# Reordering the table steps and the weighing of rows in a two-layer graph kernel on one core

## Chip, core and metric

The kernel runs on one core of a Trainium2 chip. Time is the device time of one execution in microseconds (us), and less is better. The core's engines run side by side, each through its own instruction stream in order: PE (TensorE, matrix products and transposes), DVE (VectorE), ACT (ScalarE), POOL (GpSimd) and SP (SyncE, which here only issues transfers). Transfers between the chip's DRAM (HBM) and the on-chip memories (SBUF, and PSUM for PE's results) run on 16 DMA engines.

## What is computed

There are 32 items; each is a matrix x of 512 channels by 1024 nodes. Two layers follow each other, each with a residual sum and a layer normalization over the nodes.

```python
# layer 0: attention over nodes, then a linear map and ReLU
q = einsum('c,bcn->bn', wq, x);  k = einsum('c,bcn->bn', wk, x)
scores = q[:, None, :] + k[:, :, None]
scores = where(scores > 0, scores, 0.01 * scores)
att = softmax(scores, axis=-1)
agg = einsum('bcn,bmn->bcm', x, att)
x = layernorm(x + relu(einsum('oc,bcm->bom', adj, agg) + bm[None, :, None]))
# layer 1: a linear map with W = adj * adj
x = layernorm(x + einsum('bnf,nm->bmf', x, adj * adj) + bias)
```

## The kernel before

**The attention without its 1024 x 1024 matrix.** A score is q of one node plus k of another, through a leaky ReLU, so after sorting the nodes by q the exponentials of a row split at one place: on one side they are exp(q) times a factor of the row, on the other exp(0.01 q) times another. Sums from the front and from the back of the sorted nodes therefore give every row of the attention. For an item b the steps are:

- `project` (L259): PE multiplies x by the weights and gets z = adj x with q and k as extra columns, in eight parts of 128 nodes, each in two halves; ACT copies each part into `zrow` (L275). Their PSUM tiles come from `ps_mm`, which has three buffers.
- `place` (L319), `send` (L333), `fetch` (L372): DVE counts each node's rank, POOL scatters the rows of z into a DRAM table `td` at their ranks, and SP fetches them back sorted into `zs` with eight transfers, the first six of which hold what the first weights need.
- `weigh` (L389): ACT takes exponentials of the sorted q (L398) and DVE multiplies them with triangular masks into `lq` (L406, L414), which are PE's weights for the tables. Part 0 gives the weights for table steps 0 and 1, part 1 those for all others.
- `table` (L418), nine steps: PE makes running sums of 120 sorted rows (`tp`, L426), ACT copies them out (L431), POOL and ACT carry the last sum into the next step's input (L435, L437), and SP writes the sums to `td` (L440). A step cannot start before the carry of the step before. Most steps share one PSUM buffer, `ps_t`.
- `pick` (L444): POOL gathers for 128 nodes at a time the row at its split and the two sums beside it, into `rows`; eight gathers an item.
- `shares` (`own` and `norm`), `scale`, `gain` (L456 to L504): small DVE operations and an exponential on ACT give three factors for each node; ACT scales the first row by its factor (L493), DVE adds the two others (L501, two instructions a gain).
- `turn` (L535): eight PE transposes bring 128 channels back, ACT applies bias and ReLU (L543). `join` adds x (L548) and takes statistics (`stats`, L510, L512); `root`, `shift` and `apply` normalize, on POOL (L518, L519), DVE (L525) and ACT (L531).

**Layer 1** is one level of a Strassen-Winograd scheme: `sums` (L575) builds differences of the normalized halves in parts of `rows` that are free by then, seven pairs of products (`mul`) run on PE (L592), and DVE adds them up (`read`, L604). `stats1`, `roots`, `ready` normalize the result and store it. For the last item some sums and additions run on POOL.

**The order.** Nothing is rearranged by a scheduler: the order of the calls is the order on each engine, and waits follow from the data and from buffers. `begin` and `opening` fill the pipeline, then `slot(s)` runs for s = 1 to 29. In slot s, item s+2 is projected while the tables of item s+1 (`mid`) are made, item s's last rows (4 to 7) are weighed and turned, and item s-1 (`old`) is normalized. Then `phase` runs the layer-1 products of item s, ranks and scatters item s+2, gathers rows for item s+1 and weighs its rows 0 to 3. So that the engines overlap, the calls of a slot are spread by hand over the eight projections z = 0 to 7 (L869 to L934). The first table step of item s+1 stands between the two halves of projection 4.

`end` (L936) has the last two items, 30 (`s`) and 31 (`mid`), with no projection left: the rows 4 to 7 of item 30 and the tables of item 31, the layer-1 products of item 30 (`rest`, L654, with `after(i)` called behind each product), the gathers and weighing of item 31, and `last` for its layer 1.

Of the kernel before, what the change touches and what calls it, by code (L numbers as in the profile page):

```python
# [23 lines left out]
def gat_gcn_resnorm_kernel(  # L24
# [46 lines left out]
    nc = tc.nc  # L71
# [505 lines left out]
    def layer1(b):  # L577
# [19 lines left out]
        def read(mt, half, w, m, *of):  # L597
            if (b, mt) not in vs:
                pool, tag = (xpool, "x") if b >= B - 2 else (vpool, "v")
                vs[b, mt] = pool.tile([P, N], F32, name=f"v_{b}_{mt}", tag=tag)  # L600
            x0 = ops[b, w][:, m, :] if w else vs[b, mt][:, half]
            x1 = bias_bc[:, half] if not of else vs[b, of[0]][:, of[1]]
            by = nc.gpsimd if b == B - 1 and not w else nc.vector
            by.tensor_tensor(vs[b, mt][:, half], x0, x1, ALU.add)  # L604

        mul, get = [], {}
# [47 lines left out]
    def rest(b, after):  # L654

        mul, get, reads = layer1(b)
        names = (("c1",), ("c5",), ("u2",), ("u3", "u4", "22"), ("21",), ("12",), ("11",))
        for i in range(len(mul)):
            mul[i]()
            if i == 0:  # L660
                after(-1)
                shift(0, b, CT - 1)
                apply(0, b, CT - 1)
                sums(b, ("T2", 0), ("T2", 1), ("T3", 0), ("T3", 1), ("T4", 0), ("T4", 1))
            for name in names[i // 2]:
                if b == B - 1 and i > 9:
                    get[name, i % 2]()
                elif i % 2:
                    reads(name)
            after(i)  # L670
# [198 lines left out]
    def slot(s):  # L869
# [4 lines left out]
        for z in range(NT):  # L874
            step, ot = 2 * (z - tz), z - tz
            if z == NT - 1:
                turn(s, CT - 1)
                sums(s, ("T1", 0), ("T1", 1))
            project(new, z, 0)
            if step >= 0:  # L880
                table(mid, step)
            if ot == 0:
                roots(old, 0, 1)
            if ot == 1:
                root(0, s, 0)
            if ot == 2:
                roots(old, 2, 3)
            if z == NT - 1:
                add(s, CT - 1)
            if 0 <= ot < CT - 1:  # L890
                turn(s, ot)
            if z == NT - 1:
                shift(0, s, CT - 2)
                apply(0, s, CT - 2)
            project(new, z, 1)
            if z == 0:
                shares(s, NT // 2, NT)
                scale(s, (4, 5))
                gain(s, (4, 5))
            if z == 1:  # L900
                scale(s, (6, 7))
                gain(s, (6,))
            if z == 2:
                weigh(mid, 0)
                gain(s, (7,))
            if z == 3:
                stats1(old, 0, 1)
            if step == 0:
                weigh(mid, 1)
            if step >= 0:  # L910
                table(mid, step + 1, pool=ps_mm if z == NT - 1 else ps_t)
            if step == 4:
                share(mid)
            if 0 <= ot < CT - 1:
                join(s, ot)
                if ot > 0:
                    root(0, s, ot)
            if ot == 0:
                for mt in (0, 1):
                    shift(1, old, mt)  # L920
                    apply(1, old, mt, by=nc.vector)
                    store(old, mt)
            if ot == 1:
                stats1(old, 2, 3)
            if ot == 2:
                for mt in (2, 3):
                    shift(1, old, mt)
            if new + 1 < B and z >= tz:
                load(new + 1, ot)
# [6 lines left out]
    def end():  # L936

        s, mid, old = B - 2, B - 1, B - 3
        shares(s, NT // 2, NT)
        scale(s, range(NT // 2, NT))  # L940
        gain(s, (4, 5))
        weigh(mid, 0)
        table(mid, 0)
        gain(s, (6,))
        table(mid, 1)
        gain(s, (7,))
        weigh(mid, 1)
        for ot in range(CT):
            turn(s, ot)
            if ot == CT - 1:  # L950
                sums(s, ("T1", 0), ("T1", 1))
            table(mid, 2 + ot)
            join(s, ot)
            root(0, s, ot)
        share(mid)

        def after(i):
            if i in (-1, 2, 4):
                table(mid, CT + 2 + (i + 1) // 2)
            if i in (5, 7):  # L960
                ready(old, i - 5, i - 4)
            if i in (3, 5):
                stats1(old, i - 3, i - 2)
                roots(old, i - 3, i - 2)
            if i == 5:
                for mt in range(6):
                    pick(mid, mt)
            if i in (7, 9):
                pick(mid, 6 + (i - 7) // 2)

        rest(s, after)
        shares(mid, 0, 2)
        scale(mid, (0, 1))
        own(mid, 2, 4)
        gain(mid, (0,))
        norm(mid, 2, 4)
        scale(mid, (2, 3))
        gain(mid, range(1, 4))
        shares(mid, 4, NT)
        scale(mid, range(4, NT))  # L980
        gain(mid, range(4, NT))
        for ot in range(CT):
            turn(mid, ot)
            if ot == CT - 1:
# [39 lines left out]
```

## Time and profile before

| What | Value |
|---|---|
| Median of 3 runs | 2340.5 us (2339.24 to 2347.45) |
| The profiled execution | 2344.84 us, its span 2342.9 us |
| Mean granted PE clock | 0.977 |
| Bytes moved by DMA | 548.68 MB, 234 GB/s over the span |

The span is the time from the first to the last instruction in the profile of one execution. The page also shows how the engines' work lies over the span, in 40 slices of 58.6 us; a digit is the busy share of a slice in tenths:

```profile
PE   8869999999999999999999999999999999999666
DVE  4278988988898988898898899898889889889777
ACT  2565566666556667556667655666655666755443
POOL 1334444543444543444453344454344445334333
PEclk9979999999999999999999999999999999999787
DMA  6567878777778777777777787877778787777741
```

PE is busy nearly throughout from the fourth slice on; the last three slices, about 176 us, are less filled on all engines and on the DMA. The chain of work that ended last, as shares of the span:

```profile
DVE 55%; DMA 13%; issue 10%; PE 9%; ACT 7%; POOL 5%; SPq 0%; ACTq 0%; DVEq 0%; POOLq 0%
```

The slots follow each other about every 69 us. A line of the timeline has the start, the duration, the engine, the line of the kernel, the operation, out<-in by the names of the tiles, the shapes and the count, and in brackets the idle time ahead of it with what ended it. A line of the waits has the total in us, the number of times and the longest.

### The profile page before, as it was taken

To read this page: it belongs to the slowest core of one execution; us is meant where nothing else is said; L and a number is where in the kernel's file an instruction comes from. 1 tells how busy PE (TensorE), PEld (TensorE's weight loads), DVE (VectorE), ACT (ScalarE), POOL (GpSimd) and SP (SyncE) were. 2 spreads that over 40 slices of the span, in tenths; PEclk is the share of its full clock that TensorE was granted. 3 is DMA by queue.
4 is the path that set the end of the run, shared out by engine and by line. 5 is a ranking of instruction groups with operands and counts; after the bars stand their busy time and mean duration, and the time that the engine had idled before them with its cause. 6 is when DMAs were issued, how large, how long until landed. Compare 5 with 4: busy or idle time off the path is not lost.

```text
span 2342.9 us, 30955 instructions
## 1 busy us (share of the span) xinstructions
PE 2200.9 (94%) x9521; PEld 1385.4 (59%) x9521; DVE 1995.4 (85%) x4156; ACT 1402.6 (60%) x2186; POOL 1001.9 (43%) x1299
## 2 busy tenths in 40 slices
PE   8869999999999999999999999999999999999666
PEld 7636666566666656666556665565666665666322
DVE  4278988988898988898898899898889889889777
ACT  2565566666556667556667655666655666755443
POOL 1334444543444543444453344454344445334333
PEclk9979999999999999999999999999999999999787
DMA  6567878777778777777777787877778787777741
GB/s 250 164 196 236 258 239 275 253 223 226 247 246 263 259 234 221 237 255 245 265 239 221 238 250 241 271 253 227 228 237 257 253 264 243 224 232 232 218 173 72
DMA packets 175421, 548.68 MB, mean 234 GB/s; under 512 B 24748, under 2 KB 24760, under 8 KB 175256
## 3 DMA queue, kind: packets, MB, share of 16 engines
q1 hardware_dynamic: 117888, 277.18, 39.7%
q0 software_dynamic: 57344, 269.52, 32.8%
q8 instruction: 76, 1.25, 0.2%
q14 instruction: 89, 0.73, 0.1%
q10 hardware_dynamic: 24, 0.01, 0.0%
HBM read 338.17 MB, written 208.43 MB: 233 GB/s over the span
## 4 chain that ended last, share of the span: by engine, by line
DVE 55%; DMA 13%; issue 10%; PE 9%; ACT 7%; POOL 5%; SPq 0%; ACTq 0%; DVEq 0%; POOLq 0%
DVE lt L326 13%; DMA rows<-td,idx 10%; DVE v L604 9%; DVE st L510 8%; DVE rows L501 6%; PE zp L267 5%; DVE rows L575 5%; DVE y L548 4%; PE tp L426 3%; POOL td L336 3%; DVE v L533 2%; PE op L539 2%; ACT y L531 2%; ACT y L543 1%; DVE lq L406 1%
## 5 line engine op out<-in xcount | busy, mean ns | idle before, releaser
L267 PE MATMUL zp<-wmT,x 128*128 128x257 f32 x4096 | 947.0, 383 | 2.6 <-ACT zrow L275 2.6
L267 PEld LDWEIGHTS zp<-wmT,x 128*128 128x128 f32 x4096 | 757.1, 190 | 164.0 <-issue 37.2
L435 POOL COPY zs<-ts 1x513 f32<-1x513 f32 x256 | 175.0, 683 | 803.4 <-ACT ts L431 803.1
L426 PE MATMUL tp<-zs,lq 128*64 128x257 f32 x2304 | 328.4, 400 | 83.8 <-DVE lq L406 66.2
L501 DVE SCALAR_TENSOR_TENSOR rows<-rows,ra 128x512 f32<-128x512 f32 x512 | 373.0, 750 | 35.2 <-ACT rows L493 26.1
L447 POOL DMA_INDIRECT rows<-td,idx x256 | 292.1, 1141 | 202.3 <-issue 119.4
L336 POOL DMA_INDIRECT td<-zrow,ranki x256 | 277.6, 1084 | 117.7 <-DVE ranki L331 47.9
L469 ACT ACTIVATE ac<-s 128x4 f32<-128x4 f32 (+1 forms) x65 | 13.6, 209 | 501.5 <-DVE s L468 413.6
L326 DVE SCALAR_TENSOR_TENSOR lt<-qb,zrow,first 128x1024 int8<-128x1024 f32 x240 | 307.2, 1280 | 4.3
L426 PEld LDWEIGHTS tp<-zs,lq 128*64 128x64 f32 x2304 | 150.1, 139 | 243.3 <-DVE lq L406 72.6
L431 ACT COPY ts<-tp 128x514 f32<-128x514 f32 x288 | 169.1, 587 | 193.4 <-PE tp L426 184.0
L351 ACT ACTIVATE sg<-lq,kc 128x1024 int8<-128x1024 f32 x240 | 275.8, 1149 | 6.8
L592 PE MATMUL oA<-y,adj_sb 128*128 128x512 f32 x512 | 245.1, 612 | 7.0 <-ACT y L531 4.7
L592 PE MATMUL oS<-rows,ws 128*128 128x512 f32 x512 | 225.5, 592 | 0.0
L493 ACT ACTIVATE rows<-rows,ra 128x512 f32<-128x512 f32 x256 | 167.7, 716 | 56.7 <-DVE ra L480 48.6
L275 ACT COPY zrow<-zp 128x514 f32<-128x514 f32 x256 | 148.1, 579 | 82.4 <-PE zp L267 70.9
L519 POOL TENSOR_TENSOR rs<-rs,mhalf 128x1 f32<-128x1 f32 x256 | 171.8, 671 | 21.3
L531 ACT ACTIVATE y<-y,nb,rs 128x1024 f32<-128x1024 f32 x128 | 158.7, 1240 | 27.8 <-DVE nb L525 26.3
L539 PE MATMUL op<-ident,rows 128*128 128x128 f32 x1024 | 148.2, 288 | 26.6 <-DVE rows L501 26.6
L548 DVE TENSOR_TENSOR y<-y,x 128x1024 f32<-128x1024 f32 x128 | 156.1, 1219 | 17.1 <-ACT y L543 16.9
L592 PEld LDWEIGHTS oS<-rows,ws 128*128 128x128 f32 x512 | 96.5, 189 | 123.0 <-issue 113.4
L510 DVE BATCH_NORM_STATS2 st<-y 128x6 f32<-128x512 f32 x256 | 164.2, 684 | 2.6
(109 smaller groups left out, 2544.5 us busy)
## 6 DMA issues: line engine op xcount, KB each, us to landing
x<-in_x_dram SPq DMA_DIRECT2D x128, 512.0 KB
out_dram<-v SPq DMA_DIRECT2D x126, 512.0 KB
td<-ts SPq DMA_DIRECT2D x512, 120.5 KB
zs<-td SPq DMA_DIRECT2D x64, 602.3 KB
zs<-td SPq DMA_DIRECT2D x64, 240.9 KB
zs<-td SPq DMA_DIRECT2D x96, 120.5 KB
td<-ts SPq DMA_DIRECT2D x64, 96.4 KB
td<-zs SPq DMA_DIRECT2D x8, 514.0 KB
```

What stands on the lines that cost most here:

```text
L267: nc.tensor.matmul(zp[:, h, 0:CE], xb[ct][:, nt * P : (nt + 1) * P], wmT[:, ct, h * CE : (h + 1) * CE], start=(ct == 0), stop=(ct == CT - 1),)
L326: nc.vector.scalar_tensor_tensor(lt, qs, zrow[:, nt, 0:1], first[:, o : o + N], ALU.subtract, ALU.is_lt, accum_out=rank[:, nt : nt + 1],)
L336: sc = nc.gpsimd.indirect_dma_start(out=td[:, :], out_offset=bass.IndirectOffsetOnAxis(ap=ranki[:, nt : nt + 1], axis=0), in_=zrow[:, nt, ...
L351: nc.scalar.activation(sg, qs, AF.Sign, bias=kc[:, nt : nt + 1], accum_out=sgn[:, nt : nt + 1])
L426: nc.tensor.matmul(tp[i * G : (i + 1) * G, h, 0:CE], lw[:, ks[i], :], zs[:, j, h * CE : (h + 1) * CE], start=True, stop=True,)
L447: nc.gpsimd.indirect_dma_start(out=rows[:, mt, :], out_offset=None, in_=tds[b].rearrange("(s u) c -> s (u c)", u=3), in_offset=bass.Indire ...
L501: nc.vector.scalar_tensor_tensor(u, g[:, k, i, 1 : C + 1], ra[:, k, i : i + 1], u, ALU.mult, ALU.add)
L510: nc.vector.bn_stats(st[:, h, :], t[:, h * H : (h + 1) * H])
L531: nc.scalar.activation(t, t, AF.Identity, bias=nb, scale=rs)
L548: nc.vector.tensor_tensor(t, t, xs[b][ot], ALU.add)
L592: nc.tensor.matmul(ops[b, w][:, m, :], quarters[w][:, a, m * P : (m + 1) * P], part(y, a), start=(a == 0), stop=(a == CT // 2 - 1),)
L604: by.tensor_tensor(vs[b, mt][:, half], x0, x1, ALU.add)
```

## The change

In each slot four calls are moved. The first turn of item s goes from before the second half of projection 4 to behind table step 1. The first weights of item s+1 (`weigh(mid, 0)`) go from z = 2 to z = 1, ahead of the scaling of rows 6 and 7, and gain 7 goes to z = 1 behind gain 6. The statistics of the old item's first part (`stats1(old, 0)`) go from z = 3 to z = 0, between the scaling and the gains of rows 4 and 5.

In `end`, the first weights and table steps 0 and 1 of item 31 stand ahead of the weighing of item 30's rows, the second weights and steps 2 and 3 between its gains, and steps 4 to 7 beside the turns. Step 8 and five of the eight gathers follow the first product of item 30; the first half of item 31's rows is weighed behind product 11. In the last item, the addition `u4` of the layer-1 reads goes from POOL to DVE; `22` stays on POOL.

```diff
-            by = nc.gpsimd if b == B - 1 and not w else nc.vector
+            by = nc.gpsimd if b == B - 1 and not w and half is hi and of[1] is lo else nc.vector
...
             if i == 0:
-                after(-1)
                 shift(0, b, CT - 1)
...
-            if 0 <= ot < CT - 1:
+            if 0 < ot < CT - 1:
                 turn(s, ot)
...
             if z == 0:
                 shares(s, NT // 2, NT)
                 scale(s, (4, 5))
+                stats1(old, 0)
                 gain(s, (4, 5))
             if z == 1:
+                weigh(mid, 0)
                 scale(s, (6, 7))
-                gain(s, (6,))
-            if z == 2:
-                weigh(mid, 0)
-                gain(s, (7,))
+                gain(s, (6, 7))
             if z == 3:
-                stats1(old, 0, 1)
+                stats1(old, 1)
             if step == 0:
                 weigh(mid, 1)
             if step >= 0:
                 table(mid, step + 1, pool=ps_mm if z == NT - 1 else ps_t)
+            if ot == 0:
+                turn(s, ot)
...
         s, mid, old = B - 2, B - 1, B - 3
+        weigh(mid, 0)
+        table(mid, 0)
+        table(mid, 1)
         shares(s, NT // 2, NT)
         scale(s, range(NT // 2, NT))
-        gain(s, (4, 5))
-        weigh(mid, 0)
-        table(mid, 0)
-        gain(s, (6,))
-        table(mid, 1)
-        gain(s, (7,))
+        gain(s, (4,))
         weigh(mid, 1)
+        table(mid, 2)
+        gain(s, (5,))
+        table(mid, 3)
+        gain(s, (6, 7))
         for ot in range(CT):
             turn(s, ot)
             if ot == CT - 1:
                 sums(s, ("T1", 0), ("T1", 1))
-            table(mid, 2 + ot)
+            table(mid, 4 + ot)
             join(s, ot)
             root(0, s, ot)
         share(mid)
 
         def after(i):
-            if i in (-1, 2, 4):
-                table(mid, CT + 2 + (i + 1) // 2)
+            if i == 0:
+                table(mid, NB - 1)
+                for mt in range(5):
+                    pick(mid, mt)
...
-            if i == 5:
-                for mt in range(6):
-                    pick(mid, mt)
-            if i in (7, 9):
-                pick(mid, 6 + (i - 7) // 2)
+            if i in (5, 7, 9):
+                pick(mid, 5 + (i - 5) // 2)
+            if i == 11:
+                shares(mid, 0, NT // 2)
+                scale(mid, range(NT // 2))
+                gain(mid, (0, 1))
 
         rest(s, after)
-        shares(mid, 0, 2)
-        scale(mid, (0, 1))
-        own(mid, 2, 4)
-        gain(mid, (0,))
-        norm(mid, 2, 4)
-        scale(mid, (2, 3))
-        gain(mid, range(1, 4))
-        shares(mid, 4, NT)
-        scale(mid, range(4, NT))
-        gain(mid, range(4, NT))
+        gain(mid, (2,))
+        own(mid, NT // 2, NT)
+        gain(mid, (3,))
+        norm(mid, NT // 2, NT)
+        scale(mid, range(NT // 2, NT))
+        gain(mid, range(NT // 2, NT))
```

## The prediction

> **What bounds the kernel now.** I read the page's busy shares first, then the waits of TensorE (PE) over the repeated slots, then one slot's timelines engine by engine, then the timelines of the last 145 us.
>
> ```profile
> PE 2200.9 (94%) x9521; PEld 1385.4 (59%) x9521; DVE 1995.4 (85%) x4156; ACT 1402.6 (60%) x2186; POOL 1001.9 (43%) x1299
> ```
>
> PE is nearly full, so what can be won is its idle time. The waits of PE from 202 to 2146 us, which is slots 1 to 29 (total, times, longest):
>
> ```profile
> PE tp L426 <- DVE lq L406: 37.3, 29, 1.6
> PE tp L426 <- POOL zs L435: 2.8, 5, 0.9
> PE zp L267 <- ACT zrow L275: 2.6, 7, 1.4
> ```
>
> One wait in each slot: table step 0 waits for its weights (lq), 1.29 us on average, at least 0.80 and at most 1.59. All else is 5 us in 29 slots. What makes the weights late is in the timelines of one slot, VectorE (DVE) first, then ScalarE (ACT), then PE:
>
> ```profile
> 1098.47 0.17 DVE L480 TENSOR_TENSOR ra<-ac,den 128x12 f32<-128x12 f32 x1
> 1099.43 4.44 DVE L501 SCALAR_TENSOR_TENSOR rows<-rows,ra 128x512 f32<-128x512 f32 x6 [0.79 <-ACT rows L493]
> 1103.79 0.48 DVE L406 TENSOR_TENSOR lq<-tri,w 128x128 f32<-128x128 f32 x2
> 1104.19 1.54 DVE L501 SCALAR_TENSOR_TENSOR rows<-rows,ra 128x512 f32<-128x512 f32 x2
> 1105.64 1.28 DVE L510 BATCH_NORM_STATS2 st<-v 128x6 f32<-128x512 f32 x2
> ...
> 1099.91 0.57 ACT L275 COPY zrow<-zp 128x514 f32<-128x514 f32 x1
> 1100.38 1.34 ACT L493 ACTIVATE rows<-rows,ra 128x512 f32<-128x512 f32 x2
> 1102.09 0.68 ACT L398 ACTIVATE w<-zs,bw,el 128x2 f32<-128x2 f32 x2
> ...
> 1104.13 1.28 PE L426 MATMUL tp<-zs,lq 128*64 128x257 f32 x8 [0.89 <-DVE lq L406]
> ```
>
> Call T the end of the second `shares` (1098.64 here). DVE idles 0.79 until ACT has scaled a row, does three gains, then the weights, at T+5.15 in every slot; table 0 follows at T+5.49. T itself follows from the slot's earlier work: in 22 slots DVE waited for gathered rows before it (up to 2.4 us), in the rest it came straight from other work. That work hangs on the previous tables, so it moves with PE.
>
> In the end section the lines to see are these (timelines of PE, DVE and POOL, then a row of the windows view, whose columns are length, busy time of PE, PEld, DVE, ACT and POOL, granted clock, DMA share, GB/s):
>
> ```profile
> 2216.46 2.18 PE L426 MATMUL tp<-zs,lq 128*64 128x257 f32 x8 [19.55 <-DVE lq L406]
> ...
> 2210.80 0.16 DVE L466 TENSOR_TENSOR s<-rows,kc 128x4 f32<-128x4 f32 x1 [4.35 <-DMA rows<-td,idx]
> ...
> 2282.96 5.90 DVE L501 SCALAR_TENSOR_TENSOR rows<-rows,ra 128x512 f32<-128x512 f32 x8 [0.79 <-ACT rows L493]
> ...
> 2257.92 1.16 POOL L447 DMA_INDIRECT rows<-td,idx  x1 [0.57 <-DMA out_dram<-v]
> ...
> 2197.00:2216.00 19.00, 0.00 (x0) 0.00 (x0) 12.82 (x28) 6.11 (x12) 2.72 (x3) 0.63 0.99 276
> ```
>
> PE stands 19.55 us there, since the weights come after rows that landed late; the last item's gathers begin only at 2257.92; its last gains at 2282.96.
>
> **What the Trainium skill says.** "Perfetto Trace Analysis", Optimization Strategy: find the gaps on the contended engine and make what blocks them start sooner; the first wait above is such a gap. "TensorE: Matmul & The Clock Gate", What's actually happening: an idle window of some 3.4 us halves the PE clock. The trace agrees: PE idle from 2196.9, clock 0.63 over the window shown, and table 0 takes 2.18 us against 1.28 in a slot. "SBUF — State Buffer", Who interferes with whom: a DVE instruction with two SBUF inputs contends with a GpSimd (POOL) one that reads. The trace agrees: the L414 product took 0.70 us beside a POOL copy (1110.08) and 0.29 without (2224.70). The moved gains have two such inputs. "GPSIMD Engine Reference", 3.1 Elementwise: a float32 add is 1.96 times slower on GpSimd; here 1.27 against 0.68 us (L604, 128x512).
>
> **The change part by part: slots.** On DVE one statistics step (two L510 and an L512, 1105.64 to the next at 1107.09: 1.45 us) goes ahead of the gains, and the weights ahead of gains 6 and 7. From T: the statistics begin without a wait (-0.08) and cover the 0.79; +1.45; two gains, 2 x 1.455 = 2.91; weights at T+4.28 instead of T+5.15: 0.87 us sooner. Nothing is added; the 0.79 was the only idle time.
>
> The wait that is added is ACT's. The first weights' exponentials (0.68 for both) move from behind zrow 2 to behind zrow 1, so from T+3.45 to T+1.85, where they must wait for the sixth fetch of sorted rows (zs<-td). By the trace's DMA completions this landed 1.4 to 3.6 us after T, 2.5 in the middle. Behind the exponentials stand the scales of rows 6 and 7 and zrow 2 and 3. At a landing of T+2.5: exponentials done T+3.2 (DVE needs them at T+4.28), scales T+4.5 (gain 6 needs the first at T+4.7), zrow 3 T+5.5 (the copy of table 0 is due at T+5.9). At the latest landing, T+3.6, weights are 0.05 late, gain 6 0.4, the table copy 0.7; its carry then comes 0.25 after table 1 could start. Four slots are so late: about 1 us in all.
>
> On PE the turn (1.09) goes from before projection (4,1) to after table 1. Tables 0 and 1 then stand 2.97 us apart as tables 1 and 2 do (1108.11, 1111.06, no wait); the carry is through 2.58 after table 0 (POOL copy 1106.11 + 0.60), leaving 0.4. Turn 0 would come at T+8.6; gain 7 ends T+7.6, or T+8.0 if POOL's copy holds it 0.4. The ReLU of turn 0, behind the second weights and table 1's copies, lets y0 be added 0.2 later after table 0 than now; DVE had waits of 0.61 and 0.31 at 1125 to 1126 to take that. No DMA changes its place on SP or POOL in a slot.
>
> So table 0 moves 0.87 in each slot, or as far as PE's own gap lets it: 24 slots have a gap over 0.87, five have 0.80 to 0.86. 29 x 0.87 less 0.2 less the 1 us of late slots: **-24.0 us**, and some 12 to 13 us of that wait remain, where gathered rows set T.
>
> **The end**, in the times of before (hand-laid, each instruction with its interval in the timelines). The weights follow the gains of the slot before, which end at 2206.4: the fetch landed at 2205.3, so table 0 at 2206.9 and table 1 at 2210.5 (3.57 apart at half clock, as 2216.46 and 2220.03). Table 1's copies hold ACT to 2213.8, and the exponential of `shares` is behind them: it was at 2211.39, so rows 4 to 7 are 2.5 late. Second weights are behind four scales: 2218.4; tables 2 and 3 at 2219.8 and 2223.4, turn 0 at 2225.5 (before 2221.94). Turns then follow every 3.5; y3 is added at 2239.6 (before 2237.13). That is the loss. The gain: only table 8 is left for the products, its copy, behind the normalization of y3, ends about 2245.5 (before 2250.26); 4.0 us later, as from 1133.07 to 1137.11, the first gather starts, at 2249.5 instead of 2257.92. Five gathers of 1.3 stand ahead of POOL's roots of the old item, so DVE waits for those until 2257 (before 2253.26). Then DVE is full: statistics 2.8, reads 6.0 to 2267, shares 1.5, wait 0.9, gains 0 and 1 2.9, reads 1.2, gain 2 1.5, shares, gain 3 and wait 3.7: gains 4 to 7 from 2279.0 instead of 2282.96, **-4.0 us**. The rows must be in by 2275: eight gathers at 1.9 (2271 to 2280) and four stores of about 1.3 fill 20 us, 5 us of first latency: 2275 at worst. PE's clock decides between -7 (full at 2216) and -2 (half until 2245).
>
> In the last products two adds (u4) go from POOL to DVE: POOL's four took 4.9 us from 2318.98 and DVE waited 2.41 for them. Now 0.6 on DVE and 1.25 on POOL until the first dependent read, 1.9 instead of 3.7: -1.8, of which 0.2 is lost behind DVE: **-1.6 us**.
>
> Sum: -24.0 - 4.0 - 1.6 = -29.6 on the span of 2342.9 (profiled execution 2344.84), so 2313.3. The profiled execution lies 4.3 over the median 2340.5; the same difference there gives **2311 us**.
>
> **Rivals.** (1) *Gathers hold T.* If rows land no sooner although PE moves, only slots without that wait gain: 7 x 0.83 = 5.8, with the end 5.6: 2329. For it: 22 of 29 slots waited for rows, and DMA is 93% busy from 1073 to 1104. Against: it is 63% busy from 1104 to 1142, and the gathers start at the last table's write, so they move along. Half true gives 2320. (2) *Slower: ACT stuck on the fetch.* If the sixth fetch lands later than T+4.4 (5.15 less 0.75), weights come later than now, and scales, zrow copies and gains behind them too, 1 us for each us. For 0.5% slower (+11.7) against the -5.6 of the end it takes +0.6 a slot, a landing at T+5.0: 2352. The latest now is T+3.6, and neither end of it moves against the other. (3) *The end loses*: slow clock, and stores in the way of the gathers: +3 instead of -5.6, 2319; still faster. (4) *The whole gap goes*, because DMA spreads better: all 37 and end -7: 2297.
>
> **Numbers.** Forecast 78% (2303 to 2319, with (3)); gathers hold, in part or whole, 13% (2320 to 2332, a third of it within 0.5%); (2) 5%, the milder half of it no change; (4) 4%. 0.5% is 11.7 us, about what a measurement of this kernel tells from none. Faster 0.87, within 0.09, slower 0.04. Range 2300 to 2328.
>
> **What would show it.** PE's wait for lq in slots near 12 us instead of 37; weights at T+4.3; no new PE wait at turn 0 or table 1; ACT idle on zs<-td at L398; PE's long wait at the end near 10 us; first gather some 8 us sooner against the end of slot 29. It is wrong if weights come after T+5, or table 1 or turn 0 takes the wait.

## The result and the profile after

| What | Before | After |
|---|---|---|
| Median of 20 runs each, taken together | 2340.3 us (2334.26 to 2347.45) | 2333.57 us (2327.32 to 2339.78) |
| Ratio | | 0.997, 95% interval 0.996 to 0.9979 |
| Profiled execution: its time, its span | 2344.84, 2342.9 us | 2335.49, 2333.5 us |
| Mean granted PE clock | 0.977 | 0.976 |

The change makes the kernel about 7 us faster, where 29 were forecast. The first row of the page, busy times, and the waits of PE over the slots (202 to 2140 us: total, times, longest) of the changed kernel:

```profile
PE 2201.6 (94%) x9521; PEld 1384.9 (59%) x9521; DVE 2004.2 (86%) x4151; ACT 1401.9 (60%) x2185; POOL 1044.8 (45%) x1297
```

```profile
PE tp L426 <- POOL zs L435: 14.3, 32, 1.1
PE tp L426 <- DVE lq L406: 8.6, 20, 0.7
PE zp L267 <- ACT zrow L275: 1.2, 3, 0.6
```

PE's busy time over the whole is nearly the same. The wait for the weights (lq), 37.3 us before, is down to 8.6. A wait that was 2.8 us in 5 slots is now the largest: for the carry that POOL copies into the next table step. POOL is busy 43 us longer with two instructions fewer: the carry copies (L435) take 24 us more in all, the roots (L518, L519) 22, each in the same number of instructions. One slot, DVE, then ACT, then PE (the columns are those of the timelines before):

```profile
1095.33 0.17 DVE L480 TENSOR_TENSOR ra<-ac,den 128x12 f32<-128x12 f32 x1
1095.42 1.28 DVE L510 BATCH_NORM_STATS2 st<-v 128x6 f32<-128x512 f32 x2
1096.86 2.94 DVE L501 SCALAR_TENSOR_TENSOR rows<-rows,ra 128x512 f32<-128x512 f32 x4
1099.71 0.49 DVE L406 TENSOR_TENSOR lq<-tri,w 128x128 f32<-128x128 f32 x2
...
1098.13 0.67 ACT L398 ACTIVATE w<-zs,bw,el 128x2 f32<-128x2 f32 x2 [0.79 <-DMA zs<-td]
...
1100.06 1.28 PE L426 MATMUL tp<-zs,lq 128*64 128x257 f32 x8 [0.17 <-DVE lq L406]
```

The statistics fill the 0.79 us in which DVE used to wait for ACT. The weights begin 4.2 us after `shares` ends (1095.50), and PE waits 0.17 us for them. The end (timelines of PE, DVE and POOL):

```profile
2203.45 2.25 PE L426 MATMUL tp<-zs,lq 128*64 128x257 f32 x8 [17.56 <-DVE lq L406]
...
2203.59 0.15 DVE L466 TENSOR_TENSOR s<-rows,kc 128x4 f32<-128x4 f32 x1
2274.77 5.89 DVE L501 SCALAR_TENSOR_TENSOR rows<-rows,ra 128x512 f32<-128x512 f32 x8 [0.79 <-ACT rows L493]
...
2244.89 1.14 POOL L447 DMA_INDIRECT rows<-td,idx  x1 [5.37 <-issue]
```

The long wait is still there: PE stands 17.56 us for the weights of item 31, where about 10 were forecast. Against a common mark, the start of table 0 of item 30 (2144.91 before, 2133.44 after), the last gains start at 141.3 us instead of 138.05: later, not sooner. So the 9.4 us between the two spans come from these stretches:

| Stretch | Before | After | Difference | Forecast |
|---|---|---|---|---|
| slots, table 0 of item 2 to table 0 of item 30 | 1942.2 | 1930.9 | -11.3 | -24.0 |
| from there to gains 4 to 7 of item 31 | 138.05 | 141.3 | +3.3 | -4.0 |
| from there to the end | 59.94 | 58.7 | -1.2 | -1.6 |

The start of the kernel brings the remaining 0.15. The table holds single executions: table 0 of item 2 starts anywhere from 200.4 to 204.2 us in the kernels below, whose work up to there is nearly the same, so differences of 1 or 2 us in it mean little.

**Where the slots' gain went.** PE's idle time ahead of each table step, summed over 29 slots:

| Table step | 0 | 2 | 4 | 6 | 7 | all |
|---|---|---|---|---|---|---|
| before | 37.3 | 0.5 | 0 | 0.2 | 2.1 | 40.1 |
| after | 8.9 | 1.3 | 3.0 | 0.9 | 10.6 | 24.8 |

28 us go at table 0 and 13 come back at later steps, most at tables 7 and 4. Why, is seen in a slot of the changed kernel where table 7 waits longest (timelines of DVE, POOL and PE):

```profile
1191.83 1.23 DVE L548 TENSOR_TENSOR y<-y,x 128x1024 f32<-128x1024 f32 x1 [0.31 <-ACT y L543]
...
1192.34 1.19 POOL L435 COPY zs<-ts 1x513 f32<-1x513 f32 x1
...
1193.58 1.09 PE L426 MATMUL tp<-zs,lq 128*64 128x257 f32 x8 [1.14 <-POOL zs L435]
```

The carry copy of step 6 takes 1.19 us rather than 0.60. It lies beside DVE's add of x to output 3, which ends at 1193.06, and the copy ends 0.47 us later. In the whole trace 93 carry copies run while such an add ends. Of these, 85 end 0.46 or 0.47 us after it; the other eight start in its last 0.1 us and end 0.54 to 0.59 us after it. Before, there were 34 such copies and one late starter. In the slots it was one copy at step 6 in each of the 29, where there was just enough slack (the 29 tables 7 waited 2.1 us together); after, there are 24 more at step 3 and 26 at steps 2 and 5. In the slots 31 of 232 copies took over 0.85 us before and 57 after. The means over the slots, in us from the start of table 0, show how the adds came to lie there:

| | Add of output 0 | 1 | 2 | 3 | Copy of step 3 | of step 6 |
|---|---|---|---|---|---|---|
| start, before | 6.60 | 11.09 | 17.29 | 22.48 | 12.58 | 23.14 |
| start, after | 7.50 | 11.99 | 18.48 | 23.13 | 12.64 | 23.65 |
| mean duration of the copy, before and after | | | | | 0.60, 1.06 | 1.02, 1.17 |

Counted from table 0, output 0 is added 0.9 us later and the later outputs 0.65 to 1.2. Counted from the end of `shares`, the adds of outputs 0 and 1 have not moved (12.1 and 16.6 us behind it, before and after): table 0 has come 0.93 us sooner, and the first turn, which now stands behind table 1, keeps the adds from following. The add of output 1 used to end (12.3) just ahead of the copy of step 3 (12.58); now it lies on it. One slot before, then one after (DVE, POOL, then PE's table 4, before; DVE and POOL after):

```profile
1115.18 1.22 DVE L548 TENSOR_TENSOR y<-y,x 128x1024 f32<-128x1024 f32 x1
1116.68 0.60 POOL L435 COPY zs<-ts 1x513 f32<-1x513 f32 x1 [1.38 <-ACT ts L431]
1117.81 1.09 PE L426 MATMUL tp<-zs,lq 128*64 128x257 f32 x8
...
1111.75 1.22 DVE L548 TENSOR_TENSOR y<-y,x 128x1024 f32<-128x1024 f32 x1
1112.61 0.82 POOL L435 COPY zs<-ts 1x513 f32<-1x513 f32 x1 [0.74 <-ACT ts L431]
```

"SBUF — State Buffer", Who interferes with whom, of the Trainium skill says that such a DVE instruction, with two SBUF inputs, and a POOL instruction that reads SBUF share ports under "an exclusive lock", so that one blocks the other fully. A copy that ends 0.46 or 0.47 us after the add, whenever it started beside it (85 times here), is what a lock looks like.

### The profile page after: what moved, and what is told of

It reads as the page before. It is cut to its first block, busy times and chain, and to the rows that moved or that the text cites. A ratio compares the mean times of both kernels' runs of the same rounds, so it can differ in the third digit from the quotient of the medians.

```text
span 2333.5 us, 30954 instructions
## 1 busy us (share of the span) xinstructions
PE 2201.6 (94%) x9521; PEld 1384.9 (59%) x9521; DVE 2004.2 (86%) x4151; ACT 1401.9 (60%) x2185; POOL 1044.8 (45%) x1297
## 4 chain that ended last, share of the span: by engine, by line
DVE 39%; DMA 21%; PE 15%; issue 8%; POOL 7%; ACT 6%; SPq 3%; POOLq 0%; ACTq 0%; DVEq 0%
DVE lt L326 11%; DMA zs<-td 9%; DVE v L604 8%; PE zp L267 7%; DVE st L510 6%; DMA td<-zrow,ranki 6%; PE tp L426 5%; DMA rows<-td,idx 4%; DVE rows L575 4%; DVE y L548 3%; DMA td<-ts 2%; POOL td L336 2%; SPq L384 2%; ACT y L543 2%; DVE rows L501 2%
## 5 line engine op out<-in xcount | busy, mean ns | idle before, releaser
L435 POOL COPY zs<-ts 1x513 f32<-1x513 f32 x256 | 199.2, 778 | 701.1 <-ACT ts L431 700.1
L426 PE MATMUL tp<-zs,lq 128*64 128x257 f32 x2304 | 331.1, 402 | 76.6 <-DVE lq L406 35.5
L501 DVE SCALAR_TENSOR_TENSOR rows<-rows,ra 128x512 f32<-128x512 f32 x512 | 378.3, 760 | 14.0 <-ACT rows L493 4.8
L469 ACT ACTIVATE ac<-s 128x4 f32<-128x4 f32 x64 | 13.3, 208 | 481.9 <-DVE s L468 393.7
L518 POOL TENSOR_SCALAR rs<-mv 128x1 f32<-128x1 f32 x256 | 87.3, 341 | 230.1 <-DVE mv L512 139.8
L519 POOL TENSOR_TENSOR rs<-rs,mhalf 128x1 f32<-128x1 f32 x256 | 180.3, 704 | 21.3
```

Of the source, the lines that this page charges most:

```text
L426: nc.tensor.matmul(tp[i * G : (i + 1) * G, h, 0:CE], lw[:, ks[i], :], zs[:, j, h * CE : (h + 1) * CE], start=True, stop=True,)
L435: by.tensor_copy(zs[0:1, to, 1:ZW], ts[0:1, 1:ZW])
L501: nc.vector.scalar_tensor_tensor(u, g[:, k, i, 1 : C + 1], ra[:, k, i : i + 1], u, ALU.mult, ALU.add)
L519: nc.gpsimd.tensor_tensor(rs, rs, mhalf, ALU.pow)
```

## The experiments

The theories, by the letters that the expectations use. **L**: the first turn behind table 1 makes the outputs late, and that costs the time that is missing in the slots. **F**: ACT's new wait for the fetched rows ahead of the first weights (L398, 44.4 us in 50 waits in the slots, 25 us of it ahead of the first weights and the rest ahead of the second) is what is lost. **P**, formed after the first four runs: what is lost is POOL's carry copies, because VectorE's adds hold them (ports) or because roots stand ahead of them (queue). **E**: of the changed end. Every time is a median with its ratio to before.

**The slot edits alone.** The hunk of `slot` is taken, the hunks of `end`, `rest` and `read` are not:

```diff
-            if 0 <= ot < CT - 1:
+            if 0 < ot < CT - 1:
                 turn(s, ot)
...
             if z == 1:
+                weigh(mid, 0)
                 scale(s, (6, 7))
```

> The slot edits alone, with the end of before. By the traces of before and after the slots gave 11 us (table 0 of item 2 to table 0 of item 30: 1942.2 us before, 1930.9 after) and the end took 2 us back. Theory L (late turn): the turn behind table 1 delays y0, its statistics and POOL's roots, and the carries behind those roots; 11 us faster than before, so 2329. Theory F (fetch wait): ACT's wait for the sorted rows ahead of the scales costs what is missing; the same 11 us. If it is 24 us or more faster, the end edits are what lost the time.

2332.04 us, ratio 0.996 (0.9945 to 0.9974), as both theories had it, so it does not decide between them. PE's idle time by step is that of the change: 3.8 us ahead of table 4, 10.3 ahead of table 7.

**The end alone**, with the sums u4; the slots are those of before:

```diff
     def end():
...
+        weigh(mid, 0)
+        table(mid, 0)
+        table(mid, 1)
         shares(s, NT // 2, NT)
```

> The end edits alone (with u4 on VectorE), slots of before. Theory E: the weighing of item 30's last rows stands behind the copies of table 1 on ScalarE, and those behind a fetch that lands 12 us after its issue; gains 4 to 7 of item 31 then come about 3 us later against table 0 of item 30, u4 gives 1.2 back: 2 us slower than before. The rival, that the end does gain as predicted and the slots lost: 6 us faster.

2339.3 us, ratio 0.9991 (0.9983 to 0.9999): at most 4 us less than before, neither the 2 us more of theory E nor the 6 less of its rival. The change's gain is in its slots.

**The late turn alone**, the rest as before:

```diff
-            if 0 <= ot < CT - 1:
+            if 0 < ot < CT - 1:
                 turn(s, ot)
...
+            if ot == 0:
+                turn(s, ot)
             if step == 4:
                 share(mid)
```

> Only the first turn goes behind table step 1; all else as before. Theory L: y0 is added later against table 0, tables 4 and 7 wait for POOL's carry, about 0.55 us a slot: 16 us slower than before, with table 0 still waiting 1.3 us for its weights. Theory F: no fetch wait is added, so no change (within 3 us).

2346.13 us, ratio 1.002 (1.0012 to 1.0028). A loss, as L says, but of 5 us, not 16: the wait ahead of table 7 grows from 2.1 to 5.5 us, the wait for the weights stays. Output 0 is added 0.35 us later after table 0, not 0.9: the rest comes only when the tables start sooner as well.

**The slot edits with the first turn ahead of table 1:**

```diff
+            if ot == 0:
+                turn(s, ot)
             if step >= 0:
                 table(mid, step + 1, pool=ps_mm if z == NT - 1 else ps_t)
-            if ot == 0:
-                turn(s, ot)
```

> The slot edits with one difference: the first turn stands between the second half of projection 4 and table step 1, so ahead of table 1's copies on ScalarE; end of before. Theory L: tables 4 and 7 wait as little as before (2.6 us in all slots), and most of the 0.94 us a slot comes through: 25 us faster than before. Theory F: ScalarE's wait is still there, so 11 us faster as with s1_slots.

2343.42 us, ratio 1.0008 (0.9998 to 1.0019). The waits at tables 4 and 7 are gone, as L says; but table 2 now waits 25.8 us, and all is lost again. One slot of it (DVE, POOL, PE):

```profile
1109.07 1.22 DVE L548 TENSOR_TENSOR y<-y,x 128x1024 f32<-128x1024 f32 x1
...
1109.44 1.31 POOL L435 COPY zs<-ts 1x513 f32<-1x513 f32 x1
...
1110.81 1.16 PE L426 MATMUL tp<-zs,lq 128*64 128x257 f32 x8 [0.41 <-POOL zs L435]
```

It is the same picture at another step: an add (of output 0, ending at 1110.29), a carry copy that ends 0.46 us after it, and PE waiting. Neither L nor F foresaw it; P was formed here.

**Carry copies in two halves**, with the slot edits and the end of before, so that half of a table step's matmuls need the first half alone:

```diff
-                by.tensor_copy(zs[0:1, to, 1:ZW], ts[0:1, 1:ZW])
+                for c0, c1 in ((1, CE), (CE, ZW)):
+                    by.tensor_copy(zs[0:1, to, c0:c1], ts[0:1, c0:c1])
```

> The slot edits, with the end of before, and GpSimd's copy of a table step's carry row cut in two (the first 256 columns, then the rest), so that the first four matmuls of the next table step need the first half alone. Theory P (the time that the slot edits should have brought is lost at tables 4 and 7, because GpSimd's carry copies of steps 3 and 6 start late and take 1.0 to 1.2 us rather than 0.60): TensorE's waits ahead of tables 4 and 7, 3.8 and 10.3 us in 29 slots with the slot edits alone, fall to about 5 together, the period falls from 68.88 to about 68.6 us and the time by 7 to 10 us, to about 2323 us. Theory F (ScalarE's wait for the fetched rows ahead of the first weights is what is lost): no change, 2332 us; if an instruction more on GpSimd costs what it brings, also 2332.

2322.66 us, ratio 0.9933 (0.9919 to 0.9946): as P says. The waits ahead of tables 4 and 7 fall from 14.1 to 6.4 us, where about 5 were expected. A blocked first half ends 0.25 us after the add, where a whole copy ends 0.46 after it.

**The same halves with the turn ahead of table 1:**

```diff
+            if ot == 0:
+                turn(s, ot)
             if step >= 0:
                 table(mid, step + 1, pool=ps_mm if z == NT - 1 else ps_t)
```

> As the run with the first turn between the second half of projection 4 and table 1, with GpSimd's carry copy in two halves. Theory P: the wait ahead of table 2 (25.8 us in 29 slots, from a carry copy of 1.20 us beside the two-source add of the first output) falls by about 0.5 us a slot to about 11, the time from 2343.4 to about 2329 us. Rival (the copy as a whole is waited for, or ScalarE's own carry copy of 0.62 us ends no sooner): it stays within 3 us of 2343.

2333.81 us, ratio 0.9967 (0.9958 to 0.9976). The time falls by some 10 us, of the 14 that P expected; but in the profiled execution the wait ahead of table 2 falls only from 25.8 to 22.6 us, so P's reason is not shown here. The first half is itself held until 0.25 us after the add, so it comes only some 0.2 us sooner than a whole copy. And the profiled execution, 2340.02 us, is the slowest of the 16 of this kernel, so it may not show what made the others faster.

**Adds of outputs 0 and 2 replaced** by two statistics of the same output, which have one SBUF input. This kernel and the next leave the residual sum of these outputs out:

```diff
     def add(b, ot):
         t = ys[b][ot]
+        if 0 < b < B - 2 and ot in (0, 2):
+            st = small.tile([P, NH, 6], F32, name=f"sx_{b}_{ot}", tag="st")
+            for h in range(NH):
+                nc.vector.bn_stats(st[:, h, :], t[:, h * H : (h + 1) * H])
+            return
         nc.vector.tensor_tensor(t, t, xs[b][ot], ALU.add)
```

> The slot edits, with the end of before; in the slots the adds of x to the outputs 0 and 2 are left out, and two batch-norm statistics of the same output (1.28 us against 1.22, one SBUF source rather than two) stand in their places on VectorE. If VectorE's two-source adds slow GpSimd's copies beside them (P, ports): the copies of steps 3 and 6, mean 1.04 and 1.13 us, fall to below 0.8, the wait ahead of table 7 from 10.3 us to below 4, the time by about 8 us to 2324. If the copies are late only because of the roots queued ahead of them (P, queue): durations stay above 1.0 and the time stays near 2332.

2331.11 us, ratio 0.996 (0.9947 to 0.9974): no faster than the slot edits alone, and the copies of steps 3 and 6 stay at 1.02 and 1.15 us. Read by the expectation, that is the queue. But the expectation named the wrong adds: each copy at steps 3 and 6 that was still slow lay beside an add of output 1 or 3, which this kernel keeps.

**Adds of outputs 1 and 3 replaced:**

```diff
-        if 0 < b < B - 2 and ot in (0, 2):
+        if 0 < b < B - 2 and ot in (1, 3):
```

> The slot edits, with the end of before; in the slots the adds of x to the outputs 1 and 3 are left out, and two batch-norm statistics of the same output stand in their places on VectorE (in the run with outputs 0 and 2 so treated, every copy above 0.85 us lay beside an add of output 1 or 3 that was left). P, ports: GpSimd's carry copies of steps 3 and 6 (means 1.04 and 1.13 us with the slot edits) fall to 0.60 to 0.70, the waits ahead of tables 4 and 7 from 3.8 and 10.3 us to below 1 and 4, the time by 6 to 9 us to about 2324. P, queue: the copies stay above 1.0 us and the time stays near 2332.

2318.55 us, ratio 0.9897 (0.988 to 0.9914). The copies of steps 3 and 6 take 0.60 us on the mean, 3 copies of 232 are over 0.85 us (55 with the slot edits), the wait ahead of table 4 is 0 and that ahead of table 7 2.5 us. The time is 13.5 us below the slot edits alone, more than the 6 to 9 expected. Two instructions as long together as the add (1.29 us), in its place, with one SBUF input, and the copies are free: the ports, not the queue. In one slot (POOL, DVE; L551 is the statistics):

```profile
1115.14 0.60 POOL L435 COPY zs<-ts 1x513 f32<-1x513 f32 x1
...
1114.64 1.29 DVE L551 BATCH_NORM_STATS2 sx<-y 128x6 f32<-128x512 f32 x2 [0.31 <-ACT y L543]
```

The copy lies wholly beside the statistics and takes its 0.60 us.

**Rows first, early tables.** The slots and the opening of `end` are those of before; tables and gathers come earlier; u4 and the tail are the change's:

```diff
         def after(i):
-            if i in (-1, 2, 4):
-                table(mid, CT + 2 + (i + 1) // 2)
+            if i in (-1, 0, 1):
+                table(mid, CT + 3 + i)
+            if i == 1:
+                for mt in range(5):
+                    pick(mid, mt)
```

> The slots of before, and another end: the last rows of item 30 are weighed ahead of the first weights, as before; the tables 6, 7 and 8 of item 31 stand ahead of the layer's first product and within its first two; the first five gathers come behind table 8; the sums u4 alone on GpSimd; the tail as in the change. Theory E (the end of the change lost because the weighing of the rows stood behind the copies of tables 0 and 1, not because of early tables and gathers): gains 4 to 7 of item 31 at 130 to 133 us after table 0 of item 30, against 138.1 before and 141.3 with the change; the time 5 to 8 us below before, 2333 to 2335 us. Rival (the gathers hold one another up, or the products wait for the tables): gains at 138 or later, the time within 2 us of 2340.

2337.9 us, ratio 0.9993 (0.9986 to 0.9999): the rival. Gains 4 to 7 came at 138.0 us. PE waited 8.0 us in 5 waits for carries between the turns and table 8, two tables running behind one product; product 9 gave way to product 10 at 118.4 us (113.3 before); and gathers 5 to 7 stood behind roots on POOL.

**Tables spread over the products, gathers ahead of roots:**

```diff
-            if i in (-1, 0, 1):
-                table(mid, CT + 3 + i)
-            if i == 1:
+            if i in (-1, 1, 2):
+                table(mid, {-1: 6, 1: 7, 2: 8}[i])
+            if i == 2:
                 for mt in range(5):
                     pick(mid, mt)
+            if i in (5, 7, 9):
+                pick(mid, 5 + (i - 5) // 2)
             if i in (5, 7):
                 ready(old, i - 5, i - 4)
```

> The slots of before; the end of the run before it with rows first, but with tables 6, 7 and 8 of item 31 behind the products 0, 1 and 2 (rather than 6 and 7 both behind product 0), the first five gathers behind table 8, and gathers 5, 6 and 7 each ahead of GpSimd's roots of the same step. Theory E (early gathers pay, where no product waits for a table's carry and no gather stands behind a root): product 8/9 ends at 115 to 117 us after table 0 of item 30 (113.5 before, 121.8 with the first rows-first end), the last gather is issued at 117 to 119 (122.6 before), gains 4 to 7 of item 31 come at 129 to 132 (138.05 before), and the time falls by 6 to 10 us, to 2330 to 2334. Rival (what the products lose to tables 6 to 8 is as much as the gathers win): gains 4 to 7 at 136 or later, the time 2337 to 2340.

2334.94 us, ratio 0.9967 (0.9951 to 0.9982): between the two. Product 10 follows 9 at 114.5 us, but the last gather comes at 120.8, for roots of the older item still lie between the gathers on POOL, and gains 4 to 7 at 135.2: 2.9 us sooner than before rather than 6 or more. (The 121.8 of the expectation is the end of product 11 in the run before; its product 9 gave way at 118.4.)

**The rows first in the changed end, nothing else:**

```diff
-        weigh(mid, 0)
-        table(mid, 0)
-        table(mid, 1)
         shares(s, NT // 2, NT)
         scale(s, range(NT // 2, NT))
+        weigh(mid, 0)
         gain(s, (4,))
+        table(mid, 0)
+        table(mid, 1)
```

> The change as it is, with one edit in its end: the shares and the scaling of item 30's rows 4 to 7 stand ahead of the first weights and of tables 0 and 1 of item 31, with gain 4 ahead of table 0. If the end of the change loses because the shares' exponential stands behind ScalarE's copies of tables 0 and 1: the exponential starts at 66 to 71 us after table 0 of item 30 (76.9 with the change), the first turn at 82 to 84 (87.4), gains 4 to 7 of item 31 at 137 to 139 (141.3), and the time falls by 2 to 4 us to about 2330.5. If the products wait for the tables in any case: gains 4 to 7 at 141, the time 2333.

2334.93 us, ratio 0.9969 (0.9957 to 0.9981). The steps are near what was expected: exponential at 66.7 us, first turn at 84.9 (82 to 84 was expected), gains 4 to 7 at 138.8, and 2.5 us less from table 0 of item 30 to the end (197.5 against 200.0). The time cannot tell 2.5 us from nothing: its interval and that of the change cover each other.

**Slots with halved copies, and that end:**

```diff
+            if i in (-1, 1, 2):
+                table(mid, {-1: 6, 1: 7, 2: 8}[i])
...
+                for c0, c1 in ((1, CE), (CE, ZW)):
+                    by.tensor_copy(zs[0:1, to, c0:c1], ts[0:1, c0:c1])
```

> The slots of the change with GpSimd's carry copies in two halves (2322.7 us with the end of before), and the end with tables 6 to 8 spread over the products and gathers ahead of roots. If the two add up and theory E of the end holds: 2312 to 2316 us. If the end brings only what the sums u4 bring: 2321 us.

2317.85 us, ratio 0.9889 (0.987 to 0.9908). That is above the 2312 to 2316 of theory E and below the 2321 of its rival. The two gains do add up: the product of the ratios of the two parts, 0.9933 and 0.9967, is 0.990.

**The adds kept away from the copies.** The slots of the change with whole copies, the last end, and another order on DVE; nothing is left out here:

```diff
-            if z == NT - 1:
-                add(s, CT - 1)
...
             if z == NT - 1:
                 shift(0, s, CT - 2)
+                stats1(old, 3)
+                add(s, CT - 1)
                 apply(0, s, CT - 2)
+                roots(old, 3)
...
+            if ot == 1:
+                shift(0, s, 0)
+                stats1(old, 2)
+                add(s, 1)
+                stats((0, s, 1), ys[s][1])
+                apply(0, s, 0)
+                root(0, s, 1)
```

> The slots of the change and the end of the last runs (tables 6 to 8 behind products 0 to 2, gathers ahead of roots), GpSimd's carry copies whole again; and VectorE's order in the slots changed so that no add of x to an output lies beside a carry copy: the statistics of the earlier item's rows 2 go ahead of the add of output 1, and those of its rows 3 ahead of the add of output 3, with their roots and shifts. If it is the adds of outputs 1 and 3 that hold GpSimd's copies, the copies of steps 3 and 6 take 0.60 to 0.70 us on the mean, TensorE's waits for GpSimd's carries in the slots fall below 5 us (9.5 with the copies in halves), the period is 68.2 to 68.4 us, and the time 2306 to 2312 us against 2317.9 with the copies in halves. If the later adds are late for the next product or for the roots, the time is lost there and it stays at 2316 to 2322.

2329.47 us, ratio 0.9947 (0.9927 to 0.9967). The copies of steps 3 and 6 take 0.60 us, and tables 4 and 7 wait 0 and 1.6 us: so far as meant. But table 5 now waits 23.5 us. POOL and PE in one slot; ACT had copied out the sums of table 4 by 425.42:

```profile
426.78 0.23 POOL L518 TENSOR_SCALAR rs<-mv 128x1 f32<-128x1 f32 x1 [3.61 <-DVE half L359]
427.09 0.57 POOL L519 TENSOR_TENSOR rs<-rs,mhalf 128x1 f32<-128x1 f32 x1
427.61 1.39 POOL L435 COPY zs<-ts 1x513 f32<-1x513 f32 x1
...
429.05 1.09 PE L426 MATMUL tp<-zs,lq 128*64 128x257 f32 x8 [1.50 <-POOL zs L435]
```

The copy of step 4 stands behind the root of output 1, whose statistics the new order makes later: POOL waits for DVE until 426.78 (the bracket names the DVE instruction that ended last; the statistics that the root needs, L512, end at 426.69), with a copy behind the root that could have run since 425.42. By 427.61 it meets the add of output 2 as well. One line is moved:

```diff
                 apply(0, s, 0)
-                root(0, s, 1)
...
             if ot == 2:
+                root(0, s, 1)
                 roots(old, 2)
```

> As the run before it (no add of x beside a carry copy), but with GpSimd's root of output 1 behind the carry copy of step 4 rather than ahead of it: there the copy of step 4 had stood 1.82 us behind that root, and TensorE had waited 23.5 us in 29 slots ahead of table 5, while the waits ahead of tables 4 and 7 were 0 and 1.6. If that queue is all that the new order cost: the wait ahead of table 5 goes, the waits for GpSimd's carries in the slots sum to below 5 us, the period falls from 68.95 to 68.2 to 68.4 us, and the time from 2329.5 to 2308 to 2314 us. If the later adds cost elsewhere, the period stays above 68.6 and the time above 2318.

2308.41 us, ratio 0.9855 (0.9837 to 0.9872), 1.45% below before and the fastest of all. PE's waits in its slots (206 to 2115 us), and one meeting of the copy of step 6 with DVE (POOL, DVE, PE):

```profile
PE tp L426 <- DVE lq L406: 8.4, 17, 0.7
PE tp L426 <- POOL zs L435: 7.6, 14, 1.1
```

```profile
1115.90 0.60 POOL L435 COPY zs<-ts 1x513 f32<-1x513 f32 x1 [1.65 <-ACT ts L431]
1116.67 1.08 POOL L518 TENSOR_SCALAR rs<-mv 128x1 f32<-128x1 f32 x1 [0.18 <-DVE mv L512]
...
1115.66 0.68 DVE L510 BATCH_NORM_STATS2 st<-v 128x6 f32<-128x512 f32 x1
1116.38 0.21 DVE L512 BATCH_NORM_AGGREGATE mv<-st 128x2 f32<-128x12 f32 x1
1116.50 1.17 DVE L548 TENSOR_TENSOR y<-y,x 128x1024 f32<-128x1024 f32 x1
...
1117.07 1.09 PE L426 MATMUL tp<-zs,lq 128*64 128x257 f32 x8
```

The copy ends where the add begins, and table 7 waits for nothing. The add now falls on a root (1.08 us), for which PE does not wait. The waits for carries were expected below 5 us and are 7.6 (2.2 us ahead of table 2, 2.0 ahead of 6, 3.8 ahead of 7); the period of a slot is 68.27 us, within the 68.2 to 68.4 expected.

## Why the prediction was wrong

- **The weights in the slots: right.** T+4.28 was forecast and 4.22 measured (mean), table 0 0.93 us sooner instead of 0.87, a wait of 8.6 us instead of 12 to 13 left. ACT's wait for the fetch costs next to nothing, as forecast: it makes ACT idle, not DVE. F falls: the kernel with the adds of outputs 1 and 3 replaced and the last one keep this wait (40.7 and 50.7 us in the slots) and win all the same.
- **The step that failed in the slots** is the one on the first turn: its ReLU "lets y0 be added 0.2 later after table 0 than now; DVE had waits of 0.61 and 0.31 at 1125 to 1126 to take that". The add came 0.9 us later after table 0, and later adds 0.65 to 1.2. No wait of DVE can take this, for the price is not paid on DVE: POOL's copies, which stand on the path of the tables, moved onto the adds. The prediction had named the ports and counted POOL holding a gain, but of the adds it asked only when they were done, not beside what they ran. Of the 28 us gone at table 0, 13 came back so, 11.5 of them at tables 4 and 7. When the two adds take one input, or lie elsewhere, the waits at tables 4 and 7 fall to 2.5 and 3.8 us, and the time to 2318.55 us (the end of before) and 2308.41 (the other end). The stretch of the slots is then 1912.5 and 1911.4 us, 20 to 31 below the four kernels with the slots of before (1932.4 to 1942.2): what the forecast of 24 asked for.
- **How sure the slots' numbers are.** The time says -0.4% for the slot edits alone, 6 to 13 us by the interval. Profiles of single executions scatter: the slots of before ran at 69.37, 69.22, 69.03 and 69.01 us each in four kernels that share them, those of the change at 68.96, 68.88 and 68.82. So -11.3 may flatter the change, since before's is the longest of its four. The wait ahead of table 0 scatters with it (37.3, 36.9, 33.5, 31.1 us before), so what went there is 22 to 28 us; that ahead of table 7 scatters less (2.1, 2.5, 1.8, 2.0 us before; 10.6, 10.3 and 9.5 with the slot edits).
- **The end.** The term of -4.0 reads +3.3 in the table, but most of this is not the work of the end's edits: with the slot edits and the end of before the stretch is already 140.1 us, and in the eight kernels with that end it lies between 138.05 and 141.4. From table 0 of item 30 to the last instruction the change takes 200.06 us and the slot edits alone 200.08. So the gain did not come; that the end lost is not shown. Two steps of the forecast failed. The first, "the fetch landed at 2205.3, so table 0 at 2206.9", misread the trace: 2205.28 is the landing of the third of the eight transfers. The sixth, which the first weights need, landed at 2210.98 before, and at 2202.66 after, 12.2 us after its issue, when it shared the DMA engines with the gathers of item 30's last rows. So the weights moved 1.5 us against item 30's tables, not 9.6. The second, that the exponential of `shares` would be "2.5 late", was 10.4 (76.9 instead of 66.5): rows and fetch land close together, so putting tables 0 and 1 first only puts ACT's copies ahead of the rows. DVE took up the rows at 2203.59 and then stood still (DVE, then ACT, changed kernel):

```profile
2203.98 0.16 DVE L468 TENSOR_TENSOR s<-s,tl 128x4 f32<-128x4 f32 x1
2210.57 0.17 DVE L477 TENSOR_TENSOR ra<-rows,ac 128x12 f32<-128x12 f32 x1 [6.43 <-ACT ac L469]
...
2209.08 0.59 ACT L431 COPY ts<-tp 128x514 f32<-128x514 f32 x1 [2.10 <-PE tp L426]
2209.70 0.61 ACT L437 COPY zs<-ts 1x513 f32<-1x513 f32 x1
2210.34 0.21 ACT L469 ACTIVATE ac<-s 128x4 f32<-128x4 f32 x1
```

  The exponential takes 0.21 us, and ACT idles 2.10 us ahead of table 1's copies, but the order keeps it behind them. Turn 0 came at 87.4 us instead of 77.0 and product 10 began at 120.3 instead of 113.3. The first gather came 1.6 us sooner, the last one 4.7 later: the last three stand on POOL behind four roots of item 29, two of which wait for DVE or ACT first; they end at 2257.05, 0.20 us ahead of the sixth gather; product 9 had ended 3 us before. The kernel with the rows put first shows that the order on ACT delays the exponential and the turns: 66.7 and 84.9 us there, and 66.1 to 69.1 and 76.6 to 79.6 in all the kernels that keep the order of before. What that costs the gains cannot be told: 138.8 lies within the 138.05 to 141.4 that one and the same end gives.
- **The sums u4**: -1.2 instead of -1.6; from those gains to the end the change and the seven other kernels with these sums take 58.7 us each, before and the seven others without them 59.9. They were not run alone.
- **Rivals.** The end did not bring its 5.6 us, as the third rival had it, but by another way: not the clock and the stores, but ACT's and POOL's order; a loss of 3 is not shown. That gathers hold T and that ACT sticks on the fetch did not happen: the wait for weights went as far as forecast. (The chances as written give 0.91 for faster: 0.78, two thirds of 0.13, and 0.04.)

What stays open: why PE's own work in the slots took 4.2 us longer (1902.95 against 1898.72 busy, the same 8316 instructions), which is why the stretch is only 11.3 shorter where 15.3 us of PE's idle time went; why halving the copies helped the turn ahead of table 1 by more than its waits show; how the 7 us of the change split between slots and end more finely than the intervals allow; and what the last kernel still loses at tables 2, 6 and 7.

## What to carry to other kernels

When an instruction moves, ask not only who waits for it and when it is done, but what it will run beside: an instruction of DVE with two SBUF inputs that comes to run beside a POOL copy on the critical path, here through a shift of 1 us between the two, costs more than its lateness. Where POOL carries a serial chain, lay one-input work (statistics, here) beside each link and put nothing ahead of the link in POOL's queue that waits for DVE. And before a step is placed ahead of another because its data "come first", read both landings from the DMA completions.

## What the runs showed of the hardware

The block is sharp: a carry copy that runs into the end of an add ends 0.46 or 0.47 us after it (34 of 35 copies before, 85 of 93 after; the others start in the add's last 0.1 us). Cut in halves, the blocked half ends 0.25 us after it (79 cases). A copy of 0.60 us became as long as 1.49 beside an add in the changed kernel.

It goes both ways, and the one that starts first runs on. In the last two kernels 57 carry copies start up to 0.6 us ahead of an add and run into its time: all take 0.60 us, and the add ends 1.08 us or more after the copy (it takes 1.22 where it runs free). The sharpest case, with 0.06 us between the starts (the kernel before the last; POOL, DVE):

```profile
2081.84 0.60 POOL L435 COPY zs<-ts 1x513 f32<-1x513 f32 x1
2081.90 1.62 DVE L548 TENSOR_TENSOR y<-y,x 128x1024 f32<-128x1024 f32 x1 [0.28 <-ACT y L543]
```

So in these runs a copy on the critical path need not be far from an add: it is spared where it starts ahead of it.

POOL's roots are slower beside DVE too: the `tensor_scalar` on 128x1 (L518) took 1.08 us beside the add at 1116.50 (last kernel) and 0.21 to 0.23 us where it stands free, and the power (L519) 1.43 us at 1110.44 in the changed kernel, as at 1113.87 before, against 0.57, beside two normalizations on DVE (L533, 0.81 us each, to 1111.83) which have one tensor input only.
